# First loads, last turn, sums announced singly and new ranks in a four-layer graph attention stack

## The chip, the cores and the metric

The kernel runs on one core of one Trainium2 chip. The metric is the device time of one execution in microseconds; of several runs the median counts.

## What is computed

The input x holds 128 graphs of 64 nodes with 512 features; `adj` is a mask of 64x64 for each graph. Four layers follow one another, each as `x = x + layer(relu(layernorm(x)), adj)`. Cut to what matters:

```python
# layers 0 and 2: 4 heads of 64, bias bo
q, k, v = h @ Wq, h @ Wk, h @ Wv
attn = softmax(where(adj, q k^T / 8, -max))
out = (attn v) @ Wo + bo
# layer 1: a second layernorm with gamma and beta, 8 heads of 64,
# w_qkv and w_out in place of the four weights, the diagonal always allowed
# layer 3: 8 heads of 64
m = h @ map_w.T + map_b
n = m / |m| by head;  near = (n n^T > 0.1) where both nodes are kept
p = softmax(where(allowed, (m q_w)(m k_w)^T / 8, -1e10))
A = near * p
out = relu((A (h @ gcn_map_w.T + b)) @ gcn_W.T / (sum(A) + 1))
```

All of it is in float32.

## The kernel before, in words

The 8192 tokens are cut into 16 groups (`s` = 0 to 15) of 512, four blocks of 128 tokens with two graphs each. A step is a pair of layer and group, (l, s); the steps run layer by layer, group by group, and between layers a group lies in device memory (`xs`).

A step has these stages. `loads` (from L489) brings the group's x into a tile `xin` of a ring of two, in two halves of 256 tokens; group (0,1) comes on ScalarE's DMA queue, the others on SyncE's (SP). `layernorms` (L516) runs once for each half: statistics on VectorE (L456, L458, L461, L465), a power on GpSimd (L463), then the normalizing pass on ScalarE (L472). After that the features have to lie along the partitions; tile `hT` holds the group so turned. There are three ways. A plain group is transposed by TensorE (L630) and copied out of PSUM by ScalarE (L634). A group in `by_dma` (layers 0 and 2) is moved in 16 blocks by DMAs on SP (`moves`, L590) and finished by VectorE's 32x32 transpose (L605). A group in `turned` (layers 1 and 3) is moved by copies on ScalarE (13, L554) and GpSimd (3, L551), then by VectorE (L564), and in layer 1 it gets gamma and beta (L568). Before, groups 0 and 1 of every layer are plain.

Every product with a weight is a Winograd unit of seven half-sized products in place of eight (`winograd`, L721, and `product`, L673). It needs sums of weight quarters, made once by `sums_of_a` (L364 on VectorE for the first weights, L367 on GpSimd for the others), and for every group sums T of token quarters, made by `sums_of_b` (L375 on VectorE or L378 on GpSimd). Its results leave PSUM through ScalarE copies (L690, L694, L710, or L1109 for the output product) and VectorE or GpSimd additions (L703, L714, L1093, L1114). PSUM is given out in three rings of two: `ma`, `mm` and `sc`, the last for the attention tiles.

Attention works on blocks of 64x64. `front` (L1238) makes the scores (L994), the softmax runs on VectorE, ScalarE and GpSimd (L1004 to L1036) into a tile E of a ring of two, in layer 3 also with the neighbours (L1295, L1304). Then `turns` (L1350) has each unit of E turned into a tile F by `transposed` (L1038): eight ScalarE copies (L1045) and one VectorE transpose (L1049). `attentions` multiplies F with V: L1177 in layers 0 to 2, L1336 (function `last`) in layer 3, where VectorE then adds to the residual (L1229) and SP stores to `out` (L1234). In layer 3 GpSimd adds a row to V first (`add_rows`, L910). The residual x comes on SP (L1089, or L1215 in layer 3).

The order of instructions is written out by a planner inside the kernel. Each stage is a generator (a stream) that yields what it is about to use: an engine with an assumed duration and a latency, or an event to wait for. `Order.run` always advances the stream that can start first, and among equals the one with the smaller rank, from the table RANK (one row for each kind of work, one number for each layer). The planner's events and durations only set the order in which instructions are written; on the chip each engine goes through its own list in order, and waits for the data it needs. DMAs are issued from an engine's list too, so one that waits holds up those behind it on the same queue.

At the start the ScalarE queue issues `vecs`, the weights w_qk, `bdw`, group (0,1), the weights w_vo and the row bo; SP issues the first mask and group (0,0).

Of the kernel before, what the change touches and what calls it, by code (L numbers as in the profile page):

```python
# [14 lines left out]
P = 128  # L15
D = 512
N = 64
TB = 4
NC = D // P
# [8 lines left out]
DRAIN = 0.15  # L28

RANK = {  # L30
    "load": (5.5, 5.5, 3, 5.5),
    "norm0": (4, 4, 5.5, 4),
    "norm1": (4, 4, 4, 3.5),
    "move": (5, 2, 1, 5.5),
    "turn": (3.5, 3, 1, 3.5),
    "part": (5, 5, 5, 5),
    "weight": (0.5, 6, 3.5, 1),
    "proj": (5, 5, 5, 5),
    "out": (0.5, 5, 5, 2),
    "front": (0.5, 0.5, 0.5, 1.5),  # L40
    "soft": (1.5, 4, 1, 1.5),
    "near": (0.5, 3, 3, 0.5),
    "trans": (3.5, 2, 5.5, 2),
    "att": (5, 2, 2, 5),
    "res": (2.5, 1.5, 5, 6),
    "msum": (3, 0.5, 1.5, 0.5),
    "length": (4, 5.5, 2, 1.5),
# [195 lines left out]
def gnn_stack(ctx: ExitStack, tc: tile.TileContext, a: dict, out: bass.AP):  # L243
# [61 lines left out]
    for g in range(2):  # L305
        r = slice(g * N, (g + 1) * N)
        nc.vector.memset(sel[r, g:g + 1], 1.0)
        nc.scalar.dma_start(bdw[r, r], a["gcnW3"])
    vecs = const.tile([P, 6, NC], F32, name="vecs")
    nc.scalar.dma_start(vecs, a["vecs"].rearrange("p (v c) -> p v c", c=NC))  # L310
# [58 lines left out]
    def sums_of_b(B, T, vector=False):  # L369

        for o, i0, i1 in ((T[0], B(0, 1), B(0, 0)), (T[1], B(1, 1), T[0]),
                          (T[3], B(1, 0), T[1]), (T[2], B(1, 1), B(0, 1))):
            if vector:
                yield dve(0.9)
                nc.vector.tensor_tensor(o, i0, i1, ALU.subtract)  # L375
            else:
                yield pool(1.42)
                nc.gpsimd.tensor_tensor(o, i0, i1, ALU.subtract)  # L378

    def weights():  # L380
        for key, parts in units:
            yield rank("weight", int(key[-1]))
            if key == "q1":
                yield p_ready[0, 0]
            t, w_done[key] = yield from r_w.new(f"w_{key}")
            W[key] = t
            first = key == "qk0"
            for src, dst in parts(t):
                yield ("actq", 0.5, 0.0 if first else 5.0)
                nc.scalar.dma_start(dst, src.rearrange("(c p) o -> p c o", p=P))  # L390
            if first:
                begun_w.set()
                yield ("actq", 0.0, 8.0)
                first_w.set()
                yield ("actq", 0.0, 2.0)
                yield loads_begun
            if key in ("vo0", "o1", "vo2"):
                l = int(key[-1])
                src = a[f"bo{l}"]
                bo[l], bo_done[l] = yield from r_u.new(f"bo{l}")  # L400
                yield ("actq", 0.5, 2.0)
                nc.scalar.dma_start(bo[l], bass.AP(tensor=src.tensor, offset=src.offset,
                                                   ap=[[0, P], [1, D]]))
            if key == "sem3":
                yield from gcn_fold(t)
            w_ready[key].set()
            if key == "vo0":
                yield first_t
            if key in ("vo0", "vo2"):
                yield from sums_of_a(v_part(t))  # L410
                wv_sums[int(key[-1])].set()
                t = o_part(t)
            yield from sums_of_a(t, key == "qk0")
            w_sums[key].set()

    def quarter(t, c, i):

        return t[:, 2 * i + c // 2, c % 2, :]

    def gcn_fold(t):  # L420

        raw, re_ = yield from r_qk.new("raw")
        yield ("actq", 0.5, 7.0)
# [26 lines left out]
    def scales(v):  # L450

        mv = small.tile([P, 2, 2], F32, tag="mv", name="mv")
        for t in range(2):
            st = small.tile([P, 6], F32, tag="st", name="st")
            yield dve(0.68)
            nc.vector.bn_stats(st, v[:, t, :])  # L456
            yield dve(0.17)
            nc.vector.bn_aggr(mv[:, t, :], st)  # L458
# [27 lines left out]
    by_dma = [(0, 2), (0, 3), (0, 4), (0, 5), (0, 6), (0, 7), (0, 8), (0, 9), (0, 10), (0, 11), (0, 12), (0, 13), (0, 14), (0, 15), (2, 2), (2, 3), (2, 4), (2, 5), (2, 6), (2, 7), (2, 8), (2, 9), (2, 10), (2, 11), (2, 12), (2, 13), (2, 14), (2, 15)]  # L486
    turned = [(1, 2), (1, 3), (1, 4), (1, 5), (1, 6), (1, 7), (1, 8), (1, 9), (1, 10), (1, 11), (1, 12), (1, 13), (1, 14), (1, 15), (3, 2), (3, 3), (3, 4), (3, 5), (3, 6), (3, 7), (3, 8), (3, 9), (3, 10), (3, 11), (3, 12), (3, 13), (3, 14), (3, 15)]

    def loads(steps):  # L489
        for l, s in steps:  # L490
# [3 lines left out]
            for half in range(2):  # L494
# [5 lines left out]
                if (l, s) == (0, 1):  # L500
                    if half == 0:
                        yield begun_w
                    yield ("actq", 0.5, 0.0)
                else:
                    yield load(3.9)
                (nc.scalar if (l, s) == (0, 1) else nc.sync).dma_start(
                    v, x_of(l, s)[half * H:(half + 1) * H, :].rearrange("(t p) d -> p t d", p=P))
                if (l, s) == (0, 1):
                    if half == 1:
                        loads_begun.set()  # L510
                    yield ("actq", 0.0, 8.0)
# [4 lines left out]
    def layernorms(steps, half):  # L516

        for l, s in steps:
            yield rank(f"norm{half}", l)
# [3 lines left out]
            rs = yield from scales(x)  # L523
# [7 lines left out]
    def turned_tokens(l, s):  # L531
# [4 lines left out]
        if (l, s) == (3, 1):  # L536
            yield o_taken
# [32 lines left out]
        hB[l, s] = (quarters(h), with_room(T, quarters(h)), od.event())  # L570
# [39 lines left out]
    def transposes(steps):  # L610

        for l, s in steps:
            yield rank("turn", l)
# [26 lines left out]
            yield from sums_of_b(quarters(h), hB[l, s][1], (l, s) == (0, 0))  # L640
            hB[l, s][2].set()
# [3 lines left out]
    def has_h(l, s, h):  # L645
        T, t_done[l, s] = yield from r_t.new("T")
        hB[l, s] = (quarters(h), with_room(T, quarters(h)), od.event())
        h_ready[l, s].set()
# [72 lines left out]
    def winograd(A, BT, tokens_out, out_, used, begun):  # L721

        B, T, *sums = BT
# [35 lines left out]
        for e in sums:  # L759
            yield e  # L760
# [6 lines left out]
        yield read  # L767
        yield from product(p_, A[:, 2], T[2], tokens_out, False)
# [6 lines left out]
        yield read  # L775
        yield from product(p_, A[:, 3], T[3], tokens_out, False)
# [74 lines left out]
    def map_part(s, z):  # L851
# [7 lines left out]
        z["m_sums"], z["n_ready"], z["m_used"] = od.event(), od.event(), od.event()  # L859
        od.spawn(when([z["m_ready"]], w_done["map3"] if s == NG - 1 else None), 0)  # L860
# [7 lines left out]
    def of_map(n, s, z, bias):  # L868
# [4 lines left out]
        z[f"{n}_ready"] = yield from unit(W[f"{n}3"], (quarters(z["n"]), z["T"], w_sums[f"{n}3"]),  # L873
# [23 lines left out]
    def sums_after(e, B, z, done, last):  # L897
# [5 lines left out]
        yield from sums_of_b(B, T)  # L903
        done.set()

# [145 lines left out]

    def masks(l, s):

        adj, ae = yield from r_adj.new()
        n = TB * N
        yield load(3.5)
# [94 lines left out]
    def attention(l, s):  # L1151
# [45 lines left out]
        yield from sums_of_b(ov, T, True)  # L1197
# [4 lines left out]
        used = yield from unit(wo, (ov, T, w_sums[wkey]), True, Residual(got), rank("out", l))  # L1202
# [35 lines left out]
    def front(l, s):  # L1238
# [13 lines left out]
        for u in range(len(units)):  # L1252
            z["e", u] = yield from r_e.new("E")
# [60 lines left out]
    def last(s):  # L1314
# [3 lines left out]
        for u in range(2):  # L1318
            yield z["pt_ready", u]
        yield p_ready[3, s]  # L1320
        room = []
        for u in range(2):
            room.append((yield from r_sc.new("po3")))
        for u in range(2):
# [25 lines left out]
    def turns(steps):  # L1350

        for l, s in steps:
# [3 lines left out]
            for u in range(len(units_of(l)[1])):  # L1356
                yield z["e_ready", u]
                z["pt", u] = yield from transposed(*z["e", u])
# [75 lines left out]
```

## Time and profile before

| what | us |
|---|---|
| median of 3 runs (2715.89 to 2719.55) | 2717.64 |
| the profiled execution: its time | 2716.46 |
| the profiled execution: its span | 2714.7 |
| TensorE busy | 2651.8 |
| VectorE, ScalarE, GpSimd busy | 1908.4, 1887.6, 1612.0 |
| TensorE's first instruction | 15.24 |
| end of the last Winograd product | 2689.76 |

The page adds up busy time by engine and by group of instructions. The view of waits lists, for an engine, what ended its idle time, in total, times and longest. The timeline lists instructions in order: start, duration, engine, line, operation, output and inputs; behind it in brackets is how long the engine was idle and who released it. The name of a queue (SPq, ACTq) marks the issue of a DMA, not its transfer.

### The profile page before, as it was taken

Reading aid. Unit: us, or ns where it says so; the run is one execution under the profiler, and the core shown is the slowest. Engines: PE = TensorE matmul, PEld = TensorE weight load, DVE = VectorE, ACT = ScalarE, POOL = GpSimd, SP = SyncE. Lnnn points to the kernel's source line nnn. Section 1 sums busy time; section 2 is a strip of 40 time slices with the busy share of each in tenths; the row PEclk is TensorE's granted clock in tenths of the full one; section 3 lists DMA queues with packets and bytes.
Section 4 is the critical chain, followed back from the end, with each engine's and each line's share of the span. In section 5 each row is a group of like instructions: output and inputs, shape, how many; then the busy total and the mean of one; then the engine's idle time right before and its main releaser. Section 6 shows DMA issues by size and latency. Waiting matters only on the chain.

```text
span 2714.7 us, 63736 instructions
## 1 busy us (share of the span) xinstructions
PE 2651.8 (98%) x26280; PEld 2316.3 (85%) x26280; DVE 1908.4 (70%) x2836; ACT 1887.6 (70%) x3517; POOL 1612.0 (59%) x1242
## 2 busy tenths in 40 slices
PE   7999999999999999999899999999999999999997
PEld 6888888888888888888788888888888888888886
DVE  6887677667866677656568888756787667766666
ACT  5776767678867787786467777657667776677654
POOL 4776767454544355435557777677565655566543
PEclk9999999999999999999999999999999999999998
DMA  5676552202121212212356666422422233222221
GB/s 161 165 171 161 155 158 95 101 31 88 55 71 48 69 51 79 71 48 87 107 141 158 162 160 156 126 85 85 111 65 64 72 85 100 65 65 78 73 80 44
DMA packets 396978, 267.90 MB, mean 99 GB/s; under 512 B 260496, under 2 KB 305552, under 8 KB 396688
## 3 DMA queue, kind: packets, MB, share of 16 engines
q1 hardware_dynamic: 382176, 249.37, 32.9%
q10 hardware_dynamic: 14512, 14.47, 1.7%
q8 instruction: 206, 3.38, 0.5%
q14 instruction: 84, 0.69, 0.1%
HBM read 166.77 MB, written 67.63 MB: 86 GB/s over the span
## 4 chain that ended last, share of the span: by engine, by line
PE 92%; DVE 3%; DMA 2%; ACT 1%; POOL 1%; issue 1%; SPq 0%; ACTq 0%; POOLq 0%; DVEq 0%
PE mA L673 47%; PE mC L673 24%; PE mB L673 12%; PE sc L994 4%; PE po L1177 2%; PE cos L994 1%; PE po L1336 1%; PE mmn L937 1%; DMA xres<-x 1%; PE ptr L630 0%; ACT F L1045 0%; ACT E L1016 0%; DVE sc L1004 0%; POOL xres L1093 0%; DVE mx L1010 0%
## 5 line engine op out<-in xcount | busy, mean ns | idle before, releaser
L1045 ACT COPY F<-E 32x512 f32<-32x512 f32 x768 | 473.4, 616 | 35.7 <-POOL E L1036 24.9
L1114 POOL TENSOR_TENSOR xres<-xres,u 128x512 f32<-128x512 f32 x192 | 245.6, 1285 | 160.3 <-ACT u L1109 129.2
L1093 POOL TENSOR_TENSOR xres<-xres,u 128x512 f32<-128x512 f32 x192 | 261.6, 1378 | 93.9 <-DMA xres<-x 83.2
L472 ACT ACTIVATE xin<-xin,rs 128x512 f32<-128x512 f32 x320 | 246.6, 811 | 30.4 <-DVE rs L465 28.8
L463 POOL TENSOR_TENSOR rs<-rs,mhalf 128x2 f32<-128x2 f32 x160 | 134.7, 844 | 209.4 <-DVE rs L461 197.2
L554 ACT COPY hT<-xin 32x512 f32<-32x512 f32 x364 | 224.4, 617 | 6.1
L456 DVE BATCH_NORM_STATS2 st<-xin 128x6 f32<-128x512 f32 x320 | 214.9, 672 | 9.3 <-DMA xin<-x 5.4
L690 ACT COPY v<-mA 128x256 f32<-128x256 f32 (+1 forms) x192 | 92.8, 484 | 174.9 <-PE mA L673 170.3
L1036 POOL TENSOR_TENSOR E<-E,sm 128x1024 f32<-128x1024 f32 x64 | 122.6, 1917 | 126.5 <-DVE sm L1034 104.2
L378 POOL TENSOR_TENSOR t<-hT,t 128x512 f32<-128x512 f32 x126 | 182.9, 1451 | 18.1 <-ACT hT L568 7.2
L1030 DVE TENSOR_REDUCE sm<-E 128x16 f32<-128x1024 f32 x128 | 154.7, 1209 | 8.9 <-ACT E L1023 6.7
L378 POOL TENSOR_TENSOR t<-hT 128x512 f32<-128x512 f32 x63 | 82.0, 1301 | 128.8 <-DVE hT L564 46.5
L1049 DVE STREAM_TRANSPOSE F<-F 128x1024 f32<-128x1024 f32 x96 | 118.6, 1236 | 41.0 <-ACT F L1045 40.7
L673 PE MATMUL mA<-w_vo,t 128*128 128x128 f32 (+1 forms) x768 | 140.2, 314 | 1.8 <-ACT v L690 1.1
L673 PE MATMUL mA<-hT,w_qk 128*128 128x256 f32 x512 | 128.5, 387 | 2.9 <-POOL t L378 2.8
L1109 ACT COPY u<-mA 128x512 f32<-128x512 f32 x144 | 84.3, 586 | 67.4 <-PE mA L673 60.3
L1016 ACT ACTIVATE E<-sc,mx 128x64 f32<-128x64 f32 x512 | 119.8, 348 | 15.0 <-DVE mx L1013 14.4
L673 PE MATMUL mA<-t,w_qk 128*128 128x256 f32 x512 | 124.0, 383 | 4.4 <-POOL t L378 2.2
L910 POOL TENSOR_TENSOR v<-v,gcn_row 128x512 f32<-128x512 f32 x64 | 81.4, 1304 | 70.6 <-ACT v L690 70.6
L1036 POOL TENSOR_TENSOR E<-E,f 128x1024 f32<-128x1024 f32 x32 | 61.7, 1927 | 100.0 <-DVE f L1034 88.6
L673 PEld LDWEIGHTS mA<-w_vo,t 128*128 128x128 f32 x768 | 110.5, 191 | 11.4 <-ACT v L690 1.9
L1010 DVE TENSOR_REDUCE mx<-sc 128x16 f32<-128x1024 f32 x96 | 116.9, 1218 | 2.2
(223 smaller groups left out, 7335.2 us busy)
## 6 DMA issues: line engine op xcount, KB each, us to landing
x<-xres SPq DMA_DIRECT2D x96, 512.0 KB
xin<-x SPq DMA_DIRECT2D x96, 512.0 KB
xres<-x SPq DMA_DIRECT2D x64, 512.0 KB
F<-xin SPq DMA_DIRECT2D x448, 64.0 KB
xres<-in_x SPq DMA_DIRECT2D x32, 512.0 KB
u<-rs SPq DMA_DIRECT2D x128, 128.0 KB
xres<-x SPq DMA_DIRECT2D x64, 256.0 KB
out<-xres SPq DMA_DIRECT2D x64, 256.0 KB
```

Source lines behind the costliest of these rows:

```text
L378: nc.gpsimd.tensor_tensor(o, i0, i1, ALU.subtract)
L456: nc.vector.bn_stats(st, v[:, t, :])
L463: nc.gpsimd.tensor_tensor(rs[:, 0, :], rs[:, 1, :], mhalf[:, :2], ALU.pow)
L472: nc.scalar.activation(v[:, t, :], v[:, t, :], func, bias=rs[:, 2, t:t + 1], scale=rs[:, 0, t:t + 1])
L554: nc.scalar.copy(o, v)
L673: nc.tensor.matmul(o, l, r, start=(first and m == 0 and k == 0), stop=(k == KC - 1), skip_group_check=True)
L994: nc.tensor.matmul(S[g * N:(g + 1) * N, par, col], lT[r, c, k], rT[r, c, k], start=True, stop=True)
L1030: nc.vector.tensor_reduce(o, E, AX.X, ALU.add)
L1036: nc.gpsimd.tensor_mul(E, E, sm[:, :, None].to_broadcast([P, 16, N]))
L1045: nc.scalar.copy(F[g * N + 32 * k:g * N + 32 * (k + 1), :, 32 * i:32 * (i + 1)], E[g * N + 32 * i:g * N + 32 * (i + 1), :, 32 * k:32 * (k ...
L1093: nc.gpsimd.tensor_add(xr[:, t, :], xr[:, t, :], bo[l])
L1114: nc.gpsimd.tensor_add(v, v, both(u))
```

## The change

The first group's x comes as four quarters of 128 tokens, the first DMAs on SP's queue; each quarter's statistics have an event of their own (`first_x`), and the first group's stages have the rank 0.3. The first weights come in four DMAs in place of two, all on ScalarE's queue; w_vo, the rows bo, `vecs` and `bdw` go to SP's queue, and the first mask is asked for after both halves of the group are normalized. Only the groups under `PLAIN` are transposed by TensorE: (0,0), (0,1), (1,0) and (3,0). The sums T are announced one by one (`made`), with T[2] ahead of T[3], and each product waits for its own; in `attention` they are a stream of their own. For the last step, (3,15), E lies in a tile of the x ring, its two units are turned by TensorE (`by_tensor`), and `last` takes its units one after the other. All numbers of RANK are new, and DMA issues on ScalarE now count as ScalarE's time in the plan.

```diff
+GATE = [3, 2]
+PLAIN = [2, 1, 0, 1]
 RANK = {
-    "load": (5.5, 5.5, 3, 5.5),
+    "load": (6.5, 0.3, 3, 3.5),
...
-    "move": (5, 2, 1, 5.5),
-    "turn": (3.5, 3, 1, 3.5),
-    "part": (5, 5, 5, 5),
-    "weight": (0.5, 6, 3.5, 1),
-    "proj": (5, 5, 5, 5),
-    "out": (0.5, 5, 5, 2),
-    "front": (0.5, 0.5, 0.5, 1.5),
-    "soft": (1.5, 4, 1, 1.5),
-    "near": (0.5, 3, 3, 0.5),
-    "trans": (3.5, 2, 5.5, 2),
-    "att": (5, 2, 2, 5),
-    "res": (2.5, 1.5, 5, 6),
+    "move": (6.5, 6.5, 2, 6.5),
+    "turn": (3, 1.5, 4.5, 3.5),
+    "part": (4, 1.5, 5, 5),
+    "weight": (0.3, 6.5, 0.3, 3),
+    "proj": (3.5, 5, 5, 6),
+    "out": (1.5, 5, 5, 0.3),
+    "front": (2, 3.5, 0.5, 4),
+    "soft": (0.3, 3, 1, 4.5),
+    "near": (3, 0.5, 6, 4),
+    "trans": (4, 3.5, 3, 2.5),
+    "att": (2.5, 2.5, 2, 6),
+    "res": (2.5, 2.5, 4.5, 4.5),
...
-        for o, i0, i1 in ((T[0], B(0, 1), B(0, 0)), (T[1], B(1, 1), T[0]),
-                          (T[3], B(1, 0), T[1]), (T[2], B(1, 1), B(0, 1))):
+        for i, o, i0, i1 in ((0, T[0], B(0, 1), B(0, 0)), (1, T[1], B(1, 1), T[0]),
+                             (2, T[2], B(1, 1), B(0, 1)), (3, T[3], B(1, 0), T[1])):
...
+            if i:
+                made[i].set()
...
-                yield ("actq", 0.5, 0.0 if first else 5.0)
-                nc.scalar.dma_start(dst, src.rearrange("(c p) o -> p c o", p=P))
+                src = src.rearrange("(c p) o -> p c o", p=P)
+                for c in range(0, src.shape[1], 2 if first else NC):
+                    if key == "vo0":
+                        yield load(5.5)
+                    else:
+                        yield ("act", 0.5, 0.0 if first else 5.5)
+                    (nc.sync if key == "vo0" else nc.scalar).dma_start(
+                        dst[:, c:c + 2] if first else dst, src[:, c:c + 2] if first else src)
...
+    def vectors():
+        yield load(2.0)
+        nc.sync.dma_start(vecs, a["vecs"].rearrange("p (v c) -> p v c", c=NC))
+        for g in range(2):
+            r = slice(g * N, (g + 1) * N)
+            yield load(2.0)
+            nc.sync.dma_start(bdw[r, r], a["gcnW3"])
...
+    def plain(l, s):
+
+        return s < PLAIN[l]
+
+    by_dma = [(l, s) for l in (0, 2) for s in range(NG) if not plain(l, s)]
+    turned = [(l, s) for l in (1, 3) for s in range(NG) if not plain(l, s)]
...
+                elif (l, s) == (0, 0):
+                    for t in range(2):
+                        yield load(0.0)
+                        b = 2 * half + t
+                        nc.sync.dma_start(x[:, b, :], x_of(l, s)[b * P:(b + 1) * P, :])
+                        od.spawn(lands(first_x[b], 3.4 + 1.2 * b), 0)
...
-        if (l, s) == (3, 1):
-            yield o_taken
...
+            if (l, s) == GATE:
+                yield o_taken
...
-        for e in sums:
-            yield e
+        yield sums
+        yield there[1]
         yield from product(p_, A[:, 5], T[1], tokens_out, False)
...
+    def by_tensor(E, e):
+
+        F, fe = yield from r_pt.new("F")
+        p_, pe_ = yield from r_sc.new("ptr")
+        p3 = p_.rearrange("p a (i k) -> p (a i) k", k=N)
+        for i in range(16):
+            if i % 4 == 0:
+                yield quads(0.25)
+            for g in range(2):
+                r = slice(g * N, (g + 1) * N)
+                nc.tensor.matmul(p3[r, i, :], E[r, i, :], ident[r, r], start=True, stop=True)
+        e.set()
+        yield act(1.06)
+        nc.scalar.copy(F, p3)
+        pe_.set()
+        return F, fe
...
     def masks(l, s):
...
+        if (l, s) == (0, 0):
+            yield n_ready[0, 0, 1]
...
-        yield from sums_of_b(ov, T, True)
+        there = made()
+        od.spawn(sums_of_b(ov, T, there, True), rank("att", l))
...
+        if (l, s) == (3, NG - 1):
+            spare, _ = yield from r_xin.new()
+            spare = spare.rearrange("p b d -> p (b d)").rearrange("p (u i k) -> p u i k", u=2, k=N)
+            for u in range(2):
+                z["e", u] = spare[:, u], od.event()
...
     def last(s):
...
+            if s == NG - 1:
+                yield z["pt_ready", u]
+                room.append((yield from r_sc.new("po3")))
...
-                z["pt", u] = yield from transposed(*z["e", u])
+                if (l, s) == (3, NG - 1):
+                    z["pt", u] = yield from by_tensor(*z["e", u])
+                else:
+                    z["pt", u] = yield from transposed(*z["e", u])
```

## The prediction, made before the changed kernel was run

> **What bounds the kernel now.** I read four views, from the whole to the ends. First the page: busy time by engine, and the span in 40 slices.
>
> ```profile
> span 2714.7 us, 63736 instructions
> ...
> PE 2651.8 (98%) x26280; PEld 2316.3 (85%) x26280; DVE 1908.4 (70%) x2836; ACT 1887.6 (70%) x3517; POOL 1612.0 (59%) x1242
> ...
> PE   7999999999999999999899999999999999999997
> ```
>
> TensorE (PE) is busy for all but 62.9 us. The slices that are not full are the first, one in the middle and the last, so what can be won is in those 63 us and in PE work itself; an edit on DVE, ACT, POOL or a queue counts only where PE waits for it. Second, the idle time of PE added up in stretches of 50 us (windows view): 20.8 us lie in 0 to 100, 6.1 in 200 to 700 (layer 0 to 1), 13.5 in 700 to 1400 (layer 1 to 2), 1.7 in 2600 to 2650, and 18.9 after 2690. Who ends those waits, by PE's view of waits:
>
> ```profile
> PE ptr L630 <- ACT xin L472: 15.2, 1, 15.2
> PE po L1336 <- DVE F L1049: 12.4, 2, 7.2
> PE mC L673 <- ACT u L1109: 7.9, 1, 7.9
> PE mA L673 <- POOL t L378: 5.1, 2, 2.8
> PE mC L673 <- ACT v L690: 3.8, 1, 3.8
> ```
>
> Two waits hold 27.6 of the 63 us: the first transpose waits 15.2 us for the first normalized tokens, and the last attention products (`po`, L1336) wait 12.4 us for turned weights F. Third, the timeline of the start:
>
> ```profile
> 5.86 0.69 DVE L456 BATCH_NORM_STATS2 st<-xin 128x6 f32<-128x512 f32 x1 [2.91 <-DMA xin<-in_x]
> ...
> 9.72 1.01 ACTq L402 DMA_DIRECT2D u<-in_bo  x1
> 9.95 1.42 DVE L364 TENSOR_TENSOR w_qk<-w_qk 128x512 f32<-128x512 f32 x2 [2.39 <-DMA w_qk<-in_Wk]
> 10.77 1.28 ACT L472 ACT_TABLE_LOAD   x1 [10.77 <-DVE w_qk L364]
> ...
> 12.72 0.17 DVE L461 TENSOR_SCALAR rs<-mv 128x2 f32<-128x2 f32 x1
> ...
> 14.37 2.23 ACT L472 ACTIVATE xin<-xin,rs 128x512 f32<-128x512 f32 x3 [2.32 <-DVE rs L465]
> ...
> 15.24 3.00 PE L630 MATMUL ptr<-ident,xin 128*128 128x128 f32 x12 [15.24 <-ACT xin L472]
> ...
> 18.31 2.93 PE L673 MATMUL mA<-hT,w_qk 128*128 128x256 f32 x6
> ```
>
> The statistics of the first tokens are done at 7.56, but the next step on them (L461) starts at 12.72: DVE, in program order, first waits for the weights (9.95) and makes their sums. ACT is still issuing weight DMAs until 10.73 and loads its table only then. Fourth, the timeline of the end:
>
> ```profile
> 2668.77 1.24 ACT L1045 COPY F<-E 32x512 f32<-32x512 f32 x2
> ...
> 2670.21 2.09 PE L994 MATMUL sc<-kT,qT 64*64 64x64 f32 x128
> ...
> 2691.23 5.92 POOL L910 TENSOR_TENSOR v<-v,gcn_row 128x512 f32<-128x512 f32 x4
> ...
> 2699.87 5.01 ACT L1045 COPY F<-E 32x512 f32<-32x512 f32 x8 [3.55 <-POOL E L1036]
> 2704.91 1.25 DVE L1049 STREAM_TRANSPOSE F<-F 128x1024 f32<-128x1024 f32 x1 [6.01 <-ACT F L1045]
> 2706.30 1.99 PE L1336 MATMUL po<-v,F 64*64 64x64 f32 x64 [5.27 <-DVE F L1049]
> ```
>
> The last group's scores start (2670.21) just after group 14's weights are copied out of E (2670.01), though the last product of their keys had ended at 2661.06. At the end one unit's weights are turned by eight ACT copies and a DVE transpose, 6.4 us from 2699.87 to 2706.30, with PE idle.
>
> **What the Trainium skill says.** "TensorE: Matmul & The Clock Gate", section What's actually happening: an idle TensorE falls to half clock and recovers only after some 3.4 us of work. The trace agrees: the granted clock is 0.50 at 2706 to 2709, where 64 `po` records take 2.02 us, while 128 took 2.02 earlier; the first products too take 0.43 each against 0.216 (8 in 1.73) later. "Perfetto Trace Analysis", section Transposes: use the transpose form, not a matmul with the identity. The trace bears it out in counts: L630's `transpose` leaves one record per call (128 for 8 groups of 16), a `matmul` call two (2048 at L1336 for 1024 calls). "ScalarE: Activation LUTs", section What ACT_TABLE_LOAD costs: 1283 ns; the trace has 1.28 us. "DMA: Bandwidth & Descriptors", section Issuing engines are not separate DMA queues: transfers of both queues share 16 engines. The trace shows 358 to 382 GB/s from 5 to 12 us for both queues together, so x put on a queue of its own does not land as if alone.
>
> **Start.** Quarter 0 of x is now SP's first DMA, at 0.74 in place of 1.19. Before, 512 KB of x and the weights beside it landed at 5.86, so I set the first two quarters at about 5.4; statistics of the second 0.86 (0.68 and 0.18), L461 0.17, POOL's power 0.72, L465 0.16, hand-overs 0.2: 7.5. ACT's queue keeps four weight DMAs and two of the second group (0.5 each, to about 5), then the 1.28 table load: free by 6.3, before 7.5. One ACTIVATE 0.81 and a hand-over: first transpose at 8.4 in place of 15.24. The first product followed 3.07 later; if it still does, PE starts 6.9 us earlier, with the weights there by about 8.3 (2 MB at the rates of the windows). The weight sums (4 x 0.69 on DVE) must now fit between 8 and the third product; DVE's sum from 5 to 14.5 is 1.7+2.0+2.8+1.4 = 7.9 us, so they fit. The idle 2.2 us before the first T product may stay. The moved `vecs`, `bdw`, `vo0` and `bo` loads (nine DMAs, 0.4 to 1.0 each on SP) stand behind x and ahead of nothing needed before 20: nothing; if that cover goes, up to 4 us late for group 2's load. The first mask waits for both halves and is needed after 30 us: nothing. I take 7.0 (4 to 9.5), all of it carried on, since PE is at 94 to 100% from 50 us on.
>
> **Who is turned by PE.** Groups (1,1), (2,0), (2,1) and (3,1) leave TensorE: 4 x 16 transposes at 0.109 (4 in 0.44) = 7.0 us of PE work gone. In their place: 13 ACT copies of 0.617 less 4 of 0.593 (5.6 us) and 3 POOL copies of 0.64 in each of two groups, in (1,1) four ACT passes of 0.81 with gamma and beta (L568, 3.2 us) that the transposed form leaves out; 16 SP DMAs of 0.63 (10.1 us) in each of the other two; two DVE transposes of 1.23 in all four. ACT and DVE are at 70%, so this is hidden behind other groups' products; if not, PE waits once per layer start, up to 3.5 us in all. I take 7.0 (3.5 to 7).
>
> **Tail.** By TensorE a unit costs 32 calls = 64 records of 64x64. Between half-clock `po` (64 in 2.0) and twice that (only two of the four quadrants are used) I take 2.8, then one ACT copy 1.06 and 0.6 of hand-overs: 4.5 against 6.4, a gain of 1.9 for the last unit. E in a spare x tile frees the last scores from group 14: up to 8.7 us earlier (2670.2 less 2661.5). What is late next: V. The last product ends at 2689.76, its eviction at 2690.5, POOL's four row sums take 5.4 to 5.9, so `po` cannot start before 2696.2; two cold units 4.0, evictions 1.4, stores and landing 5.1 (2709.6 to 2714.7): 2706.7, a floor for the gain of 8.0 us. The lowered ranks of layer 3's front, soft and near give part back. I take 6.5 (2 to 9).
>
> **Sums announced singly, ranks searched anew.** These change the order in which instructions are written, not their number. PE idles there 21.6 us in 100 to 2600; I take zero change, bounds -8 to +14. Each switch between 64x64 and full products costs some 0.5 us (idle 0.33, and 1.93 for a product of 1.73), and a finer or coarser mix of them lies within these bounds. The singly announced sums also let a product be written ahead of a T that is late: in PE's strict order everything behind it waits. GATE compares a tuple with a list, so it is never true and that wait does not exist; before, the one in `turned_tokens` was not reached either (group (3,1) was plain): nothing.
>
> **Sum.** 7.0 + 7.0 + 6.5 = 20.5 us off the profiled 2716.46 (span 2714.7 and 1.8 around it) gives 2696; the median shown is 1.2 higher, so 2697.
>
> **Rivals.** (A) As summed: 2697, own range 2690 to 2704, chance 0.55. (B) The new order also removes the 7.9 us wait at 1298, when the residual load stood on SP behind twelve `F<-xin` moves from 1277.98 to 1295.51, or as much elsewhere: 9 off, 2688, chance 0.20. For it: these stalls are single events; against: the same queue gets more moves. (C) The gains at the ends come, but a new wait at a layer start gives half back (11): 2708, chance 0.18. (D) Slower: the moves of (2,0) and (2,1), 32 more on SP, stand ahead of layer 1's residual loads; at the 17.5 us that twelve waiting moves took, POOL's sums, ACT's `u` buffers and then PE wait. Each group of moves can add 11.5 (16 x 0.72, as eight in 5.78 at 39.82), both 23: 2697 + 23 = 2720, chance 0.07. It decides once over 20.5 us of moves stand before a residual that is due. Against: SP idles most of 1180 to 1273.
>
> 0.2% (5.4 us) is about what a measurement here tells from no change: below 2712.2 is faster. A, B and 0.13 of C are faster, 0.05 of C is the same, D is slower: 0.88, 0.05, 0.07. The range reaches from B's best, 2684 (9.5 + 7 + 9 + 8 = 33.5 off), to C's worse end, 2711; it leaves out D and a little of C.
>
> **What would show it.** First transpose at 8 to 9 and first product near 11.4; L630 with 64 records, `F<-xin` moves 480, L1045 with 752; last scores before 2662 on the old clock, at most 18 us from the last full product to the end; PE idle after 1280 not above 13. If the first product still waits for weights at 15 or later, or PE's idle time between 100 and 2600 exceeds 35 us, the prediction is wrong.

## The result, and the profile after

The changed kernel takes 2676.98 us (median of 4 runs, 2672.95 to 2678.70) against 2716.89 us: a ratio of 0.9849, 95% interval 0.9832 to 0.9867. It is faster by 39.9 us; the prediction was 20 us faster, 2697, with a range that ended at 2684. The direction was right, the size half of what came, and the time lies below the range.

The page of the changed kernel, as far as it answers to the lines of before:

```profile
span 2675.2 us, 63987 instructions
...
PE 2630.3 (98%) x26344; PEld 2308.6 (86%) x26344; DVE 1853.5 (69%) x2842; ACT 1889.7 (71%) x3517; POOL 1591.0 (59%) x1248
...
PE   7999999999999999999999999999999999999998
```

The span is 39.5 us shorter, but TensorE idles only 18.0 us less (44.9 in place of 62.9). The other 21.5 us are busy time, although it has 64 records more. The middle slice that was not full is full now. By the view of waits of the changed kernel:

```profile
PE ptr L672 <- ACT xin L494: 11.3, 2, 8.9
PE mA L714 <- ACT v L731: 7.8, 9, 2.6
PE mA L714 <- DVE t L375: 3.2, 4, 2.3
PE mA L714 <- POOL t L378: 3.2, 1, 3.2
PE sc L1038 <- issue: 3.1, 2, 2.5
```

(The lines have moved: L672 is L630 of before, L714 L673, L731 L690, L1410 L1336.) The two large waits have shrunk: the first transpose waits 8.9 us in place of 15.2, and the 12.4 us of the last `po` products have become two waits of 1.1. The single wait of 7.9 us for `u` is gone. The timeline of the start:

```profile
4.83 0.38 ACTq L548 DMA_DIRECT2D xin<-in_x  x1
...
8.88 1.97 PE L672 MATMUL ptr<-ident,xin 128*128 128x128 f32 x8 [8.88 <-ACT xin L494]
...
11.51 0.41 ACTq L548 DMA_DIRECT2D xin<-in_x  x1
11.95 0.58 ACT L676 COPY hT<-ptr 128x512 f32<-128x512 f32 x1 [2.43 <-DMA w_vo<-in_Wv]
...
14.48 2.93 PE L714 MATMUL mA<-hT,w_qk 128*128 128x256 f32 x6
```

The first transpose comes at 8.88, the first full product at 14.48 (18.31 before). The copy between them stands in ScalarE's list behind the issue of group (0,1)'s second half, which does not go out until 11.51. By 100 us the lead is gone. After its first transpose TensorE still waits 5.6 us there in the kernel before and 11.9 us in the changed one. The four longest of these waits are for the second half's normalized tokens (2.5), for T from VectorE (2.3) and from GpSimd (3.2), and for a copy of v (2.6). The end:

```profile
2657.81 2.08 PE L1106 MATMUL ptr<-ident,xin 64*64 64x64 f32 x64 [0.57 <-DVE xres L1293]
...
2662.77 2.08 PE L1106 MATMUL ptr<-ident,xin 64*64 64x64 f32 x64 [0.57 <-POOL xin L1080]
...
2664.90 1.01 ACT L1109 COPY F<-ptr 128x1024 f32<-128x1024 f32 x1 [3.96 <-PE ptr L1106]
...
2665.97 1.16 PE L1410 MATMUL po<-v,F 64*64 64x64 f32 x64 [1.11 <-ACT F L1109]
2668.86 1.29 DVE L1293 SCALAR_TENSOR_TENSOR xres<-po,xres 128x512 f32<-128x512 f32 x2 [3.61 <-DMA xres<-x]
```

A unit's turn now takes 2.08 us on TensorE and 1.01 on ScalarE. The last products end near 2667.1, and VectorE's last additions then wait for the residual's load until 2668.86. The first of the last two `po` products, at 2661.04, was released by GpSimd's row sums for V (L954), the limit that the prediction had named next.

To see where the 39.5 us went I cut both profiled executions into stretches of 5 us (windows view) and added up two things: TensorE's idle time, and busy time times the part of the clock that was not granted, called slow clock here. Busy time less slow clock is busy time at full clock. I also counted, in the list of TensorE's instructions, the stretches of 64x64 products between full ones.

| | before | after | difference |
|---|---|---|---|
| idle, first 100 us | 20.8 | 20.8 | 0.0 |
| idle, from 100 us to 30 us before the end | 23.2 | 12.6 | -10.6 |
| idle, last 30 us | 18.8 | 11.5 | -7.3 |
| slow clock while busy | 10.5 | 1.5 | -9.0 |
| 64 transposes of 0.109 fewer | | | -7.0 |
| 128 records of `by_tensor` (2 x 2.08) | | | +4.2 |
| what is left of busy time | | | -9.7 |
| stretches of 64x64 products | 158 | 116 | -42 |

The rows in us add up to -39.4. Of the 9.0 us of slow clock, 2.0 belong to the tail, where the last products of before ran at half clock. The rest of three rows, some 27 us, is a gain that the prediction did not forecast: less idle time in the middle, less slow clock there, and what is left of busy time, beside which stand 42 stretches fewer. (The profile's record of the clock begins 21 us into the span before and 19 us after. The first products, slow in both, lie ahead of it and are not in the row of slow clock.) How idle time and slow clock go together is seen at the stall of 7.9 us, in the windows of the kernel before (the first four columns: stretch, its length, TensorE busy, its weight loads; then DVE, ACT, POOL, granted clock, DMA share, GB/s):

```profile
1300.00:1305.00 5.00, 0.00 (x0) 0.00 (x0) 2.39 (x4) 0.54 (x1) 4.91 (x5) 0.62 0.01 2
1305.00:1310.00 5.00, 3.95 (x9) 3.20 (x10) 4.30 (x4) 1.48 (x3) 4.68 (x5) 0.50 0.01 3
1310.00:1315.00 5.00, 5.00 (x21) 4.27 (x20) 3.90 (x5) 1.65 (x2) 4.84 (x7) 0.86 0.17 62
```

After the wait TensorE works at half clock until about 1311. These three stretches hold 3.95 x 0.50 and 5.00 x 0.14, together 2.7 us of slow clock, on top of the wait.

### The profile page after: what moved, and what is told of

It reads as the page before. It is cut to its first block, busy times and chain, and to the rows that moved or that the text cites. A ratio compares the mean times of both kernels' runs of the same rounds, so it can differ in the third digit from the quotient of the medians.

```text
span 2675.2 us, 63987 instructions
## 1 busy us (share of the span) xinstructions
PE 2630.3 (98%) x26344; PEld 2308.6 (86%) x26344; DVE 1853.5 (69%) x2842; ACT 1889.7 (71%) x3517; POOL 1591.0 (59%) x1248
## 4 chain that ended last, share of the span: by engine, by line
PE 91%; DMA 2%; DVE 2%; SPq 2%; ACT 1%; issue 1%; POOL 1%; DVEq 0%; ACTq 0%; POOLq 0%
PE mA L714 47%; PE mC L714 23%; PE mB L714 12%; PE sc L1038 3%; PE po L1240 2%; PE cos L1038 1%; PE po L1410 1%; SPq L630 1%; PE mmn L981 1%; DMA F<-xin 1%; DMA w_vo<-in_Wv 0%; ACT E L1060 0%; SPq L548 0%; DMA adj<-in_adj 0%; DMA w_k<-in_Wk 0%
## 5 line engine op out<-in xcount | busy, mean ns | idle before, releaser
L1177 POOL TENSOR_TENSOR xres<-xres,u 128x512 f32<-128x512 f32 x192 | 247.5, 1295 | 415.7 <-ACT u L1172 389.6
L1089 ACT COPY F<-E 32x512 f32<-32x512 f32 x752 | 462.6, 615 | 23.3 <-POOL E L1080 12.4
L1156 POOL TENSOR_TENSOR xres<-xres,u 128x512 f32<-128x512 f32 x192 | 252.9, 1335 | 25.6 <-DMA xres<-in_x 13.8
L594 ACT COPY hT<-xin 32x512 f32<-32x512 f32 x390 | 240.1, 616 | 7.2
L731 ACT COPY v<-mA 128x256 f32<-128x256 f32 (+1 forms) x192 | 92.1, 479 | 136.5 <-PE mA L714 133.4
L485 POOL TENSOR_TENSOR rs<-rs,mhalf 128x2 f32<-128x2 f32 x160 | 117.4, 737 | 71.8 <-DVE rs L483 48.2
L714 PE MATMUL mA<-w_vo,t 128*128 128x128 f32 (+1 forms) x768 | 141.3, 316 | 4.1 <-ACT v L731 2.6
L378 POOL TENSOR_TENSOR t<-hT 128x512 f32<-128x512 f32 x63 | 92.9, 1475 | 79.7 <-DVE hT L604 54.8
L714 PE MATMUL mA<-hT,w_qk 128*128 128x256 f32 x512 | 132.5, 385 | 4.3 <-ACT v L731 4.2
L731 ACT COPY qk<-mA 128x512 f32<-128x512 f32 x96 | 56.2, 585 | 111.2 <-PE mA L714 107.9
L591 POOL COPY hT<-xin 32x512 f32<-32x512 f32 x90 | 55.7, 618 | 131.3 <-ACT xin L494 128.8
L714 PEld LDWEIGHTS mA<-w_vo,t 128*128 128x128 f32 x768 | 115.0, 192 | 15.9 <-ACT v L731 2.8
L954 POOL TENSOR_TENSOR v<-v,gcn_row 128x512 f32<-128x512 f32 x64 | 80.8, 1294 | 79.0 <-ACT v L731 79.0
L714 PE MATMUL mA<-t,w_qk 128*128 128x256 f32 x512 | 121.7, 380 | 5.5 <-POOL t L378 3.2
```

The costliest lines, as they stand in the source:

```text
L594: nc.scalar.copy(o, v)
L714: nc.tensor.matmul(o, l, r, start=(first and m == 0 and k == 0), stop=(k == KC - 1), skip_group_check=True)
L731: nc.scalar.copy(o, p3)
L1089: nc.scalar.copy(F[g * N + 32 * k:g * N + 32 * (k + 1), :, 32 * i:32 * (i + 1)], E[g * N + 32 * i:g * N + 32 * (i + 1), :, 32 * k:32 * (k ...
L1156: nc.gpsimd.tensor_add(xr[:, t, :], xr[:, t, :], bo[l])
L1177: nc.gpsimd.tensor_add(v, v, both(u))
```

## The experiments

My theory after the result was that the order paid: fewer switches between 64x64 and full products, fewer and shorter stalls and so less slow clock. The rivals were that the named parts paid, or that switching costs nothing. Times are medians; "above" and "below" mean the changed kernel's 2676.98 unless something else is said, and ratios are to the kernel before on the same chip.

**The new ranks alone.** In the kernel before:

```diff
-    "load": (5.5, 5.5, 3, 5.5),
+    "load": (6.5, 0.3, 3, 3.5),
...
-    "length": (4, 5.5, 2, 1.5),
+    "length": (5, 5, 0.3, 5),
```

> The kernel before with the new RANK table and nothing else. Theory (the order is what paid: TensorE switches less often between 64x64 and full products, 116 stretches of 64x64 products in place of 158, and meets fewer long stalls, each of which also cost half clock afterwards): the 42 switches at 0.23 us give 9.7, and of the 21.6 us idle and 9 us clock loss between 100 and 2600 more than half goes: 2690 to 2698 against 2717. Rival (the named parts paid, the new ranks by themselves little): 2709 or above.

2755.75 us, ratio 1.0143 (1.0129 to 1.0157): the theory missed by the sign; the rival's bound (2709 or above) holds, but a loss was not in it. It has 116 stretches, as the changed kernel, but idles 99.9 us. By its view of waits:

```profile
PE ptr L630 <- ACT xin L472: 15.2, 1, 15.2
PE po L1336 <- DVE F L1049: 13.7, 2, 10.6
PE po L1336 <- DVE E L1020: 13.4, 3, 6.1
```

So the new table is no better table as such. Busy time at full clock did fall, 2641.3 to 2633.9, 0.18 us for each of the 42 stretches; 37.0 us more idle time and 8.4 us more slow clock outweigh it. The theory had to be mended: the table may fit one plan only.

**The price of a switch.** 128 small full products were added to layer 3, either four ahead of each unit's neighbour products, or one ahead of each quarter of them:

```diff
-            yield from scores(C, z["n"], z["n"], 4, blocks)
+            yield from scores(C, z["n"], z["n"], 4, blocks, True)
...
                     yield quads(0.242)
+                    if fill:
+                        for _ in range(1):
+                            nc.tensor.matmul(S[:, 0, 448:512], ident, ident[:, 0:N],
+                                             start=True, stop=True)
```

(In the first of the two, `if fill and b == 0 and c == 0` and `range(4)`.)

> The changed kernel with 128 added full products of 64 columns in layer 3 (each writes a place that the next product overwrites; it computes nothing that is used), four at a time ahead of each unit's neighbour products: 132 stretches. Work of 256 records at 0.054 us = 13.8 us more and 16 switches: about 2694. It is the reference for the next run.

> The same 128 added products, but one ahead of each quarter of the neighbour products: 228 stretches in place of 132, with the same instructions. Theory (0.2 to 0.25 us for each stretch): 19 to 24 us above the run with the products together. Rival, the price of the prediction (0.5 us each): 48 us above. Rival without a price of switching: 0 to 3.

2714.22 us (0.9995, 0.9988 to 1.0001) together, 2740.72 (1.0088, 1.0074 to 1.0102) spread. The pair has the same instructions, and busy time of TensorE, from the two pages, the first of the products together, the second of them spread:

```profile
PE 2663.0 (98%) x26600; PEld 2342.4 (86%) x26600; DVE 1851.1 (68%) x2842; ACT 1889.9 (70%) x3517; POOL 1589.2 (59%) x1248
```

```profile
PE 2696.0 (98%) x26600; PEld 2361.2 (86%) x26600; DVE 1849.1 (67%) x2842; ACT 1889.7 (69%) x3517; POOL 1589.5 (58%) x1248
```

26.5 us for 96 stretches more is 0.28 us each, a little above the 0.20 to 0.25 expected and about half of the prediction's 0.5; idle time is 48.3 and 45.1, so it is busy time that grows (29.3 us at full clock). The prediction had counted 0.33 us of idle time in its 0.5. In the timeline of before that is idle time of the weight loads (PEld), not of the products:

```profile
2689.76 1.96 PEld L1336 LDWEIGHTS po<-v,F 64*64 64x64 f32 x128 [0.33 <-issue]
2689.77 2.10 PE L1336 MATMUL po<-v,F 64*64 64x64 f32 x128
```

At 0.28 the change's 42 stretches are worth 11.8 us, and the new ranks alone had brought 7.4: the 9.7 us left in the table lie between. The single records of the two traces say where the time lies. At full clock a 128x256 product adds 0.22 us to busy time behind another one, 0.41 as the first behind 64x64 products and 0.47 as the first after idle time; a 64x64 record adds 0.01, or 0.20 as the first behind full ones. What such first records after a switch cost beyond ordinary ones is 60.9 us in all before and 45.5 after. So the switches account for more than the remainder, and other records, those after idle time among them, took some 6 us of it back.

The products together came out 20 us above the 2694 expected: busy time at full clock rose by 31.7, so an added record cost about 0.106 us ((31.7 - 16 x 0.28) / 256), twice the price I had worked out, and about that of a record of 128 columns (0.109).

**Old parts in the changed kernel.** First the old ranks of layer 0; then the old start, in which the plan also counts ScalarE's DMA issues as before; then `PLAIN = [2, 2, 2, 2]`; then a plan in which the first product with a token sum waits for all announcements:

```diff
         yield sums
-        yield there[1]
+        for i in (1, 2, 3):
+            yield there[i]
```

> The changed kernel with the old ranks for layer 0 alone (137 stretches of 64x64 products in place of 116). Theory of switches: 21 x 0.23 = 4.8 us slower, about 2682, and layer 0 with other stalls on top, up to 2690. Rival (the number of switches is without weight): within 2 us of 2677.

> The changed kernel with the old start: x of the first group by halves, w_vo, bo, vecs and bdw on ScalarE's queue, the first mask at once, no rank of its own for the first group. Theory (the start won 3.8 us at the first product, and both kernels have idled 20.8 us by 100 us, so it was given back): 0 to 4 us slower than the changed kernel, 2677 to 2681. Rival, the prediction's step (7 us carried to the end): 2684.

> The changed kernel with groups 0 and 1 of every layer transposed by TensorE again (64 records more). Prediction's step: 7.0 us slower, 2684. Rival (the other ways to turn cost waits of their own at the layer starts): within 3 us of 2677.

> The changed kernel, but in the plan the first product with a token sum waits for all three announcements, as before. 127 stretches in place of 116. Theory of switches: 11 x 0.23 = 2.5 us slower, and the layer starts a little later: 2679 to 2684. Rival (single announcements only change the plan, and what the chip waits for is the data): within 1.5 us of 2677.

| | us | ratio to before (95%) | idle 100 us to tail | slow clock | stretches |
|---|---|---|---|---|---|
| changed kernel | 2676.98 | 0.9849 (0.9832 to 0.9867) | 12.6 | 1.5 | 116 |
| old ranks, layer 0 | 2696.39 | 0.9920 (0.9906 to 0.9933) | 24.8 | 7.1 | 137 |
| old start | 2699.25 | 0.9946 (0.9932 to 0.9961) | 31.4 | 17.0 | 114 |
| old turn | 2714.84 | 1.0002 (0.9993 to 1.0011) | 33.8 | 10.8 | 117 |
| sums together | 2722.90 | 1.0032 (1.0020 to 1.0043) | 42.3 | 13.4 | 127 |

Idle time and slow clock are those of the one profiled execution; of the old start it was the slowest of six (2709.79 us). Each part undone costs 19 to 46 us, far more than any expectation, and together (126 us) more than three times what all parts bring. That cannot be the worth of the parts one by one. In three of the four some 10 us of idle time lie between 1750 and 2000, at the change from layer 2 to layer 3 (0.5 in the changed kernel), wherever the edit was made. In the old turn, busy time at full clock is 2637.3 against 2628.8: 8.5 us for 64 transposes and a stretch more, near the prediction's 7.0; the other 29 us are stalls and slow clock.

**The plan's numbers.** Three runs leave every instruction as it is and change one assumed duration, so that only the written order differs. The first puts back a number that the change itself had set, a part of it that neither its description nor the prediction named; the other two are numbers that the change left alone:

```diff
-                yield pool(1.35)
+                yield pool(1.42)
                 nc.gpsimd.tensor_tensor(o, i0, i1, ALU.subtract)
```

```diff
-                yield act(0.6)
+                yield act(0.61)
                 nc.scalar.copy(o, p3)
```

```diff
-                yield act(0.21)
+                yield act(0.22)
                 nc.scalar.activation(E[:, i, :], S3[:, i, :], AF.Exp, bias=mx[:, i:i + 1], scale=0.125)
```

> The changed kernel with one number of the plan put back: a token sum on GpSimd counts 1.42 us in place of 1.35. No instruction is added or removed, only the order in which they are written. Theory (the new ranks fit one complete plan, and any change in the plan's inputs deals the stalls between the layers anew): 8 to 40 us slower, with idle time of TensorE between 100 us and the tail above 20 in place of 12.6. Rival (the parts undone in the earlier runs were themselves worth 20 to 45 us): within 3 us of 2677.

> The changed kernel with ScalarE's copy out of PSUM counted 0.61 us in place of 0.60 in the plan, a number that the change never touched; no instruction is added or removed. Theory (ranks fitted to one plan): 8 to 40 us slower. Rival: within 3 us of 2677.

> The changed kernel with the exponential of layers 0 and 2 counted 0.22 us in place of 0.21 in the plan; no instruction is added or removed. A third draw for the theory that the new ranks fit one plan: 8 to 80 us slower than 2677, idle time of TensorE between 100 us and the tail above 20. Rival (the two draws before were unlucky): within 5 us of 2677.

2728.37 (1.0044, 1.0029 to 1.0059), 2753.29 (1.0132, 1.0117 to 1.0146) and 2699.69 us (0.9941, 0.9928 to 0.9955): 51, 76 and 23 us above. The rival fails in all three; the first two also lie above the 8 to 40 us expected. A copy taken for 0.61 us in place of 0.60 costs nearly twice what the whole change brings. That kernel idles 99.9 us and loses 20.4 to slow clock, with 120 stretches; by its view of waits:

```profile
PE mA L714 <- POOL t L378: 16.2, 4, 6.2
PE mA L714 <- ACT hT L608: 13.6, 2, 12.2
PE ptr L672 <- ACT xin L494: 11.2, 2, 8.7
PE po L1240 <- DVE F L1093: 5.6, 2, 5.4
```

Three of these rows are new stalls, the longest of 5 to 12 us; the third row is the start. The kernel's busy time at full clock is 2636.1 us, 7.3 above that of the changed kernel, with only four stretches more: TensorE starts again after idle time 55 times in place of 36, and each such first product is longer too, so the count of stretches alone does not give the busy time. The three runs bear out the mended theory: the ranks fit one complete plan, and each of these small changes of its inputs dealt the stalls anew.

**Parts undone in the same plan.** Where an edit keeps TensorE's order, it can be priced by itself. The first two below keep TensorE's order to the last instruction; the third differs only in that the 64 calls of `by_tensor` are gone. The start undone on the chip alone:

```diff
-                        nc.sync.dma_start(x[:, b, :], x_of(l, s)[b * P:(b + 1) * P, :])
+                        if t == 0:
+                            nc.sync.dma_start(v, x_of(l, s)[half * H:(half + 1) * H, :].rearrange(
+                                "(t p) d -> p t d", p=P))
...
-                    (nc.sync if key == "vo0" else nc.scalar).dma_start(
+                    nc.scalar.dma_start(
```

(`vecs`, `bdw` and the first bo likewise.) Then the second half of group (0,1) issued by SP:

```diff
-                (nc.scalar if (l, s) == (0, 1) else nc.sync).dma_start(
+                (nc.scalar if (l, s, half) == (0, 1, 0) else nc.sync).dma_start(
```

and the last group turned by copies:

```diff
-                if (l, s) == (3, NG - 1):
-                    z["pt", u] = yield from by_tensor(*z["e", u])
-                else:
-                    z["pt", u] = yield from transposed(*z["e", u])
+                z["pt", u] = yield from transposed(*z["e", u])
```

> The changed kernel with the first part undone on the chip alone: x of the first group in two halves in place of four quarters, and w_vo, bo, vecs and bdw issued by ScalarE again, while the plan and TensorE's order stay those of the changed kernel. Theory (other engines bound the first 100 us, the start is given back): idle time of TensorE in the first 100 us 20 to 23, total 2676 to 2681. Rival, the prediction's step (7 us carried on): 2682 to 2685.

> The changed kernel with the second half of group (0,1) issued by SP in place of ScalarE, at the same place of the written order; TensorE's order is the same to the last instruction. ScalarE's first copy out of PSUM (11.95) no longer stands behind an issue that waits until 11.51. Expected: first copy by 10, first full product at 12 to 12.5 in place of 14.48. Theory (the start is given back by 100 us, other engines bound that stretch): idle time of TensorE in the first 100 us stays at 20 to 21, total within 1.5 us of 2677. Rival, the prediction's step (what the start wins is carried on): 2.4 us faster.

> The changed kernel with the last group's two units turned by copies and VectorE again (E stays in the spare x tile). Theory: the last unit's turn is on the path that ends last; 6.4 us in place of 3.2 (2662.77 to 2665.97): about 3 us slower, 2680. Rival (GpSimd's row sums for V or the stores set the end): under 1 us slower.

The start undone: 2677.89 us (0.9858, 0.9844 to 0.9871), no difference. Its timeline of TensorE (L674 is the changed kernel's L672, L716 its L714):

```profile
9.12 1.97 PE L674 MATMUL ptr<-ident,xin 128*128 128x128 f32 x8 [9.12 <-ACT xin L494]
...
13.41 2.62 PE L716 MATMUL mA<-hT,w_qk 128*128 128x256 f32 x6
```

With halves the first transpose comes at 9.12 in place of 8.88 and the first full product even earlier, 13.41. So the 6 us of the first transpose came neither from the quarters nor from the queues. What is left of the change there is the order (statistics and normalization ahead of the weight sums and of the other loads) and the weights in four DMAs; no run separates the two. And since the early start stays in this run, it does not test whether its lead is carried on. The run with the old start does, in another plan: TensorE starts at 15.15 there and has idled 21.6 us by 100 us. SP issuing the second half: 2677.31 us (0.9852, 0.9839 to 0.9865), no difference either. The copy came at 10.08 in place of 11.95, but the product did not follow: VectorE's list had the statistics of that next group, not landed before 11.88, ahead of this group's L487, and the first product came at 14.71. The expected 12 to 12.5 was a miss: one wait gave way to the next, so this run does not test the rival either.

Turned by copies: 2681.28 us (0.9874, 0.9862 to 0.9887), 4.3 above where 3 were expected. The executions of the two kernels overlap (2677.07 to 2684.97 against 2672.95 to 2678.70), but the trace agrees: from the last full product to the end it has 22.4 us in place of 20.0. So the price is some 2 to 4 us. The last unit in its timeline, copies to product:

```profile
2662.87 5.00 ACT L1089 COPY F<-xin 32x512 f32<-32x512 f32 x8 [1.31 <-POOL xin L1080]
...
2667.91 1.25 DVE L1093 STREAM_TRANSPOSE F<-F 128x1024 f32<-128x1024 f32 x1 [1.59 <-ACT F L1089]
2669.30 1.98 PE L1410 MATMUL po<-v,F 64*64 64x64 f32 x64 [4.32 <-DVE F L1093]
```

6.4 us from weights to product, against 3.2 in the changed kernel (2662.77 to 2665.97), and the product itself at half clock (1.98 in place of 1.16) after 4.32 us in which TensorE was idle.

**The last loads.** The last group's residuals in the free x tile (with the second half of group (0,1) on SP, as above), and then their loads issued by ScalarE as well:

```diff
-            v, e = yield from r_xres.new()
+            if s == NG - 1:
+                if u == 0:
+                    both_x, _ = yield from r_xin.new()
+                v, e = both_x[:, 2 * u:2 * u + 2, :], od.event()
+            else:
+                v, e = yield from r_xres.new()
...
-                nc.sync.dma_start(x3[s2 * N:(s2 + 1) * N], by_half(x_of(3, s), 2 * u, s2))
+                (nc.scalar if s == NG - 1 else nc.sync).dma_start(
+                    x3[s2 * N:(s2 + 1) * N], by_half(x_of(3, s), 2 * u, s2))
```

> As the run before, and the last group's two residuals are loaded into the other free x tile, so that they need not wait for the stores of group 14. In the changed kernel VectorE's last additions wait for these loads (3.61 us of idle time, ended by the load, while the products had ended 1.7 us earlier). Theory (the loads set the end of the tail): the end comes 1.5 to 2.5 us earlier, 2673 to 2676. Rival (the next limit, POOL's division or the copies, holds it): no gain from it.

> As the run with the residuals in the free x tile, with their loads issued by ScalarE, so that they do not stand behind group 14's stores in SP's list. Theory (the loads' place in SP's list, not the tile, set the end): VectorE's last additions start right after the last products, 1.5 to 2.5 us earlier; total 2674 to 2677. Rival (ScalarE's issues now hold up its own last copies): no gain.

2679.12 (0.9861, 0.9848 to 0.9874) and 2675.99 us (0.9852, 0.9838 to 0.9865). The first misses: the loads still stand behind group 14's stores in SP's list, and VectorE's last additions wait 3.20 us for them. With ScalarE as issuer that wait is 1.48 us, but total and interval cannot be told from the changed kernel; whether this version is faster stays open. No version clearly below the changed kernel was found. There is no run with the old ranks for all four layers in the changed kernel.

Five kernels (the changed one, the start undone, SP issuing, and these two) have the same order of TensorE's records. They take 2675.99 to 2679.12 us, and idle 11.3 to 13.5 us between 100 us and the tail. Their slow clock, 1.5 to 4.5 us, shows how far a single execution can be trusted for that row: the 1.5 of the changed kernel is the lowest of the five.

## Why the prediction was wrong

**The step that failed** reads: "These change the order in which instructions are written, not their number. PE idles there 21.6 us in 100 to 2600; I take zero change, bounds -8 to +14." The order was not worth zero but some 27 us, and three terms of the step were off. The idle time in that window fell from 21.6 to 12.6 us, by 9.0, a little beyond the bound. Slow clock was left out, although the prediction had cited it for the tail: before, each of the three longest stalls of the middle was followed by 3.4 to 10.2 us at half clock, and with them went about 7 us. And the switches were taken to lie within the bounds without being counted, for their number cannot be read from the diff; they fell by 42 stretches, and 9.7 us of busy time went with them. Bounds from the idle time alone were too narrow on both sides: the runs with one number of the plan changed span 54 us.

That the direction came right is in part luck, for the reason given did not carry it: two of these three runs have every part that the prediction priced, and are slower than the kernel before.

**The start** (7.0 predicted): the first transpose was right (8.4 predicted, 8.88 measured), the first product 3 us late, and "all of it carried on" was wrong: by 100 us both kernels have idled 20.8 us. The plans that I ran idle 19.0 to 22.3 us there, whether TensorE starts at 8.9 or at 15.2. No engine is busy throughout this stretch (VectorE 64 us of 100, ScalarE 55, GpSimd 58), so these seem to be chains from engine to engine; which of them sets the 20 us I did not find, and that the early start is worth nothing in this plan was not tested with TensorE's order kept. The error was to read 94 to 100% busy as proof that TensorE alone sets the pace.

**Transposes** (7.0): right in TensorE's work. 64 records of 0.109 us are gone, and putting them back, busy time at full clock rose by 8.5 us. What the other ways to turn cost in waits was not measured by itself, since putting the transposes back changes the plan.

**The tail** (6.5): from the last full product to the end 20.0 us (2655.21 to 2675.2) against 24.9, a gain of 4.8, inside its bounds, though the 18 us that it gave as a sign were not reached. At the last unit the turn by TensorE saves more than I took (3.2 us in place of 1.9, since 64 records took 2.08 and not 2.8). The last additions then wait 1.7 us for the last residual's load behind group 14's stores, which the prediction did not name; but the run with most of this wait gone is not clearly faster, so what holds the rest of the gain stays open.

**Rivals and signs.** B named the stall of 7.9 us at 1298, and it is gone, but B gave the order 9 us in all. C and D did not come: the changed kernel's largest wait in the middle is 2.5 us. The counts of records came as forecast (L630, now L672, with 64; 480 moves; 752 copies). Idle time after 1280 fell from 35.5 to 16.8 us, not to 13.

So of the sum of 20.5 us, the 7 at the start did not come, the tail brought 4.8 of 6.5, and some 27 us of the order were not in it.

What stays open: whether another plan of the parts would do as well without the new ranks, and what the single announcements are worth, since undoing them changes the plan. That the ranks fit this plan is shown by what a change of it costs; how they were found is not on record. The share of each of the 27 us is read from the traces; no run takes one of them away alone.

## What to carry to other kernels

Where a planner writes the order, a new table of ranks has no price part by part: count what can be counted (switches between tile shapes, long stalls with the slow clock after them), and give the rest a range as wide as small changes of the plan's numbers make it, here from 2677 to 2753 us. Undoing one part in such a kernel measures a new plan and not the part; keep the order and undo the part on the chip alone. An earlier start is a gain only if the work behind it was waiting for nothing else.

## What the runs showed of the hardware

A stretch of 64x64 products between full ones costs TensorE about 0.28 us, in and out together (26.5 us for 96 stretches more). It stands in the busy time of the first records, and the view of TensorE's waits shows nothing of it. The first 128x256 product after idle time adds 0.47 us in place of 0.22. An added full product of 64 columns cost about 0.106 us a record, near the 0.109 of a record of 128 columns. A stall of 7.9 us brought 2.7 us of slow clock after it. A DMA issue can hold up its engine's compute: ScalarE's copy came at 11.95 behind an issue that went out at 11.51, and at 10.08 when that issue was moved to SP's queue.
